# A state space stage on one core: where the scans' factors lie, who multiplies by C, and when TensorE makes the product with B

## The chip, the cores and the metric

The kernel runs on one core of a Trainium2 chip. The metric is the device time of one execution in microseconds (us), the median of several runs. A core has five engines that work side by side, each through its own queue in order: TensorE (PE, matrix products; its weight loads are listed as PEld), VectorE (DVE), ScalarE (ACT, functions such as exp), GpSimd (POOL) and SyncE (SP, which here issues the transfers). SBUF is the large on-chip memory, PSUM the small one that TensorE writes to. Semaphores order the engines among themselves.

## The reference

A two-layer model on an input of 16 sequences x 512 positions x 256 channels. The first layer is a feed-forward block with blockwise four-bit quantisation, a state space block and the same feed-forward block again; the second has two low-rank expert blocks around an attention block. The change lies in the state space block alone:

```python
xz = hidden_states @ W_in
x, z = jnp.split(xz, 2, axis=-1)            # 512 inner channels each
x = silu(conv(x) + conv_b)                  # 4 taps along the sequence
proj = x @ W_x
dt_low, Bm, Cm = ...                        # 16 columns each
dt = softplus(dt_low @ W_dt + b_dt)
A = -exp(A_log)                             # 512 x 16 states
def step(h, inputs):                        # along the 512 positions
    h = exp(dt_t[..., None] * A) * h + (dt_t * x_t)[..., None] * B_t[:, None, :]
    y = einsum('bds,bs->bd', h, C_t)
    return h, y
y = (ys + x * D) * silu(z)
return y @ W_out
```

## The kernel before

The stage goes through the 16 sequences (called batches here) one after the other. In each it walks over four groups c of 128 inner channels, called blocks c0 to c3, and in each block over eight steps k = 0 to 7; so a batch has 32 steps and the stage 512. A step holds 32 channels x 2 times 4 states on the 128 partitions, and 2 x 512 positions along the row: a tile of 128 x 1024. Steps go in pairs q = k // 2.

A step needs four things:

- **Factors** exp(dt A): two ACT instructions (`factors`, recorded by the helper at L480). They go to a tile that `factors_at` picks: one of two tiles in PSUM, `das` (da), or one of three in SBUF, `sides` (ds). Steps 2 to 5 take ds, the others da.
- **The product with B**, dt x B. For q = 0, 1 and 3 POOL makes it (`make_bx`, L483, tile bx in SBUF). For q = TQ = 2, steps 4 and 5, TensorE makes it in PSUM (`turn_bx`, 64 small products, rows da<-diag,dT), into the da tile that those steps do not need for factors.
- **The scan** h = factor x h + product, one VectorE instruction along the row (L979). After a scan of steps 4 and 5, VectorE sets the first column of the da tile back to zero (L985).
- **The product with C**: by POOL where `other` holds (steps 0, 1 and 3, and step 5 in c0 and c2; there h is the SBUF tile hs, and the result g is written at L483), else by VectorE (L486; there h is the one PSUM tile h).

TensorE adds the g of each pair over the states into the PSUM tile y (`accumulate`, rows y<-g,fold; the due step is written in `due`); for q = 0 the skip term D u comes first (y<-u,dskd). When the four pairs are in, VectorE multiplies y into zs (`finish_mult`) at step 0 of the next block.

Between all that, the preparation of the next batch is threaded in as a generator, `prepare`, which is advanced in each step up to the count in `PREPARED`: transposes of the input (xT), the products with W_in (p<-xT,w_in), the convolution as four products with diagonal matrices (p<-xp,cwd), silu of u, W_x, the transposes of the projection, W_dt, softplus of dt, POOL's dt u, the z half with its silu, transposes of dt u (dT), normalisation of the next input (xn), and the output product of the batch before (`out_half`, tile o). Each piece of TensorE's is copied from one PSUM buffer (tag mm) by ACT before the next piece may start. ACT changes its function tables for silu and softplus and back.

All engines take their instructions of this stage in the order in which the program records them (keep_in_program_order). The tables `FACTORS` (for which later step factors are made; the entries at the front of a step or at its end), `PRODUCTS` (for which later step bx is made), `PIECES` (how many of the eight copies of dt and dt u from DRAM, ds<-dd, are issued in a step) and `PREPARED` set that order by hand. SP issues the transfers: dd<-dt (to DRAM), ds<-dd (spread over states), bc<-bd (rows of B and C).

Of the kernel before, what the change touches and what calls it, by code (L numbers as in the profile page):

```python
# [9 lines left out]
F32 = mybir.dt.float32  # L10
# [6 lines left out]
P = 128  # L17
NB, SEQ, D = 16, 512, 256
# [19 lines left out]
def macaron_kernel(  # L38
# [430 lines left out]
    def mamba_phase(w, src, dst):  # L469
        with tc.tile_pool(name="m1", bufs=1) as m1, tc.tile_pool(  # L470
            name="m2", bufs=2
        ) as m2, tc.tile_pool(name="m_da", bufs=1, space=PSUM) as ps_da, tc.tile_pool(
            name="m_h", bufs=1, space=PSUM
        ) as ps_h, tc.tile_pool(name="m_y", bufs=1, space=PSUM) as ps_y, tc.tile_pool(
            name="m_ps", bufs=1, space=PSUM
# [12 lines left out]
            def pe(out, **kw):  # L488
                tc.keep_in_program_order(nc.tensor.matmul(out, **kw))  # L489
# [5 lines left out]
            a_neg, dskd, cwd, xps = w["a"], w["dskd"], w["cwd"], w["xp"]  # L495
            fold = w["fold"]
            NP = NS // 2
            NQ = NP // 2
            TQ = 2
# [4 lines left out]
            das = []  # L504
# [2 lines left out]
                nc.vector.memset(da[:, :, 0:1], 0.0)  # L507
                das.append(da)
            sides = []
            for i in range(3):  # L510
                da = m1.tile([P, 2, SEQ], F32, name=f"ds{i}")
                nc.gpsimd.memset(da[:, :, 0:1], 0.0)
                sides.append(da)
            diag = m1.tile([P, 4, NC4, P], F32, name="diag")

            state, xns, xos, zss, rows, norms, bds = {}, {}, {}, {}, {}, {}, {}
# [332 lines left out]
            def where(t):  # L849
                return t // STEPS, t // NP % NDC, t % NP  # L850

            PIECES = ((4, 4, 0, 0), (4, 2, 2, 0), (4, 2, 2, 0), (0, 0, 4, 4))
            PREPARED = (
                (2, 4, 4, 4, 4, 5, 7, 8), (9, 11, 11, 12, 12, 13, 14, 15),
                (16, 18, 18, 19, 21, 23, 25, 27), (30, 32, 33, 34, 35, 37, 39, 40),
            )
            FACTORS = ((1, 2), (2,), (2,), (2,), (), (1,), (1,), (1,))
            PRODUCTS = ((3,), (), (4,), (4,), (4,), (), (3,), (3,))
            bxs, ys, done = {}, [], []

            def run_later():
# [4 lines left out]
            def make_bx(t):  # L866
                b, c, k = where(t)
                if b < NB and k // 2 != TQ:
                    bx = m2.tile([P, 2, SEQ], F32, name="bx", tag="bx", bufs=3)
                    B = rows[b, k // 2][:, :1, :]  # L870
                    pool(
                        bx, spread[b, c, k % 2][:, :, 1, :],
                        B.to_broadcast([P, 2, SEQ]), ALU.mult,
                    )
                    bxs[t] = bx
# [13 lines left out]
            def turn_bx(t):  # L889
                b, c, k = where(t)  # L890
                if b < NB and k // 2 == TQ:
                    bx, dT = das[t % 2], state[b][1][c // 2]
                    for j in range(2):
                        at = c % 2 * P + 64 * (k % 2) + 32 * j
                        for n in range(NC4):
                            for i in range(4):
                                pe(
                                    bx[32 * i : 32 * i + 32, j, n * P : (n + 1) * P],
                                    lhsT=dT[:, n, at : at + 32], rhs=diag[:, i, n, :],
                                    start=True, stop=True,  # L900
                                )

            def accumulate(b, c, q, gs):
                if q == 0:
                    ys.append(ps_y.tile([P, SEQ], F32, name="y", tag="y"))
                    u = state[b][0][c // 2][:, c % 2, :]
                    for i in range(0, P, 32):
                        pe(
                            ys[0][i : i + 32, :], lhsT=dskd[i : i + 32, c, :],
                            rhs=u[i : i + 32, :], start=True, stop=False,  # L910
                        )
                for i in range(4):
                    pe(
                        ys[0][32 * i : 32 * i + 32, :], lhsT=fold,
                        rhs=gs[i // 2][:, i % 2, :], start=False, stop=(q == NQ - 1),
                    )
                if q == NQ - 1:
                    done.append((b, c, ys.pop()))
# [22 lines left out]
            for _ in range(4):  # L941
                next(rest)
            def factors_at(t):
                n, k = divmod(t, NP)
                return sides[(4 * n + k - 2) % 3] if 2 <= k <= 5 else das[k % 2]

            def factors(t):

                b, c, k = where(t)
                if b < NB:  # L950
                    q, p = k // 2, k % 2
                    da = factors_at(t)
                    for j in range(2):
                        g = 4 * c + 2 * p + j
                        act(
                            da[:, j, 1:], spread[b, c, p][:, j, 0, 1:],
                            AF.Exp, scale=a_neg[:, g, q : q + 1],
                        )

            factors(0)  # L960
            due, pair = {}, []
            for t in range(STEPS * NB):
                b, c, k = where(t)
                s = t % STEPS
                if s == 0:
                    prepared = 0
                    ahead = prepare(b + 1) if b + 1 < NB else close()
                    stat = stats(b + 2) if b + 2 <= NB else iter(())
                if k not in (1, 2, 3):
                    for n in FACTORS[k][:1]:  # L970
                        factors(t + n)

                other = k in (0, 1, 3) or k == 5 and c % 2 == 0
                if other:
                    h = m2.tile([P, 2, SEQ], F32, name="hs", tag="hs", bufs=2)
                else:
                    h = ps_h.tile([P, 2, SEQ], F32, name="h", tag="h")
                turned = k // 2 == TQ
                tc.keep_in_program_order(nc.vector.tensor_tensor_scan(  # L979
                    flat(h), flat(factors_at(t)), flat(das[k % 2] if turned else bxs.pop(t)),  # L980
                    0.0, op0=ALU.mult, op1=ALU.add,
                ))
                if turned:
                    tc.keep_in_program_order(
                        nc.vector.memset(das[k % 2][:, :, 0:1], 0.0)  # L985
                    )

                if t in due:
                    accumulate(*due.pop(t))
                if k == 2:  # L990
                    turn_bx(t + 2)
                if k == 4:
                    turn_bx(t + 1)
                if s == 2:
                    load_out(b - 1)
                if s == 17:
                    load(b + 2)
                if 20 <= s < 24:
                    next(stat, None)

                if k == (0, 0, 0, 2)[c]:
                    steps = fetch_steps(*divmod(b * NDC + c + 1, NDC))
                for _ in range(PIECES[c][k] if k < 4 else 0):
                    next(steps, None)
                run_later()
                if b and s == 0:
                    fetch(b, NQ - 1)
                if c == NDC - 1 and k in (2, 4, 6):
                    fetch(b + 1, k // 2 - 1)
                if t < 4:  # L1010
                    for _ in range(2):
                        next(rest, None)
                else:
                    for _ in range(min(3, PREPARED[c][k] - prepared)):
                        next(ahead, None)
                        prepared += 1
                for n in FACTORS[k][k in (0, 4, 5, 6, 7):]:
                    factors(t + n)
                g = m2.tile([P, 2, SEQ], F32, name="g", tag="g", bufs=4)
                C = rows[b, k // 2][:, 1:, :].to_broadcast([P, 2, SEQ])  # L1020
                if k == 0 and done:
                    finish_mult(*done.pop())
                if other:
                    pool(g, h, C, ALU.mult)
                else:
                    vec(g, h, C, ALU.mult)
                for n in PRODUCTS[k]:
                    make_bx(t + n)
                if s == STEPS - 3:
                    diags = diagonals(b + 1)  # L1030
                    next(diags, None)
                if s >= STEPS - 3:
                    next(diags, None)
                pair.append(g)
                if k % 2:
                    due[t + 1 + other] = (b, c, k // 2, pair)
                    pair = []
                if s == STEPS - 1:
                    for _ in ahead:
                        pass  # L1040
# [733 lines left out]
    with tc.tile_pool(name="mw", bufs=1) as mw:  # L1774
        with tc.tile_pool(name="x", bufs=1) as xp, tc.tile_pool(
            name="fw", bufs=1
# [23 lines left out]
    with tc.tile_pool(name="fw2", bufs=1) as fw, tc.tile_pool(  # L1800
        name="ln2", bufs=2
# [70 lines left out]
```

## Time and profile before

| what | value |
|---|---|
| median of 3 runs | 4398.21 us (4396.62 to 4403.94) |
| the profiled execution: its time, its span | 4394.14 us, 4392.4 us |
| state space stage, from the first scan to the last zs product | about 629.5 to 2573.5 us of the span |
| busy from 1500 to 1800 us (300 us) | PE 245.5, DVE 268.9, ACT 193.5, POOL 272.2 |
| granted clock of TensorE in that stretch | 0.94 |
| VectorE product g<-h,bc (x288) | 1.22 us |
| POOL bx<-ds,bc (x384), g<-hs,bc (x224), mean | 2.62 us, 2.77 us |
| ACT factor, one of two per step, da / ds | 0.69 / 0.71 us |
| ACT table load in the stage (x169) | 1.28 us |

The page lists the span in 40 slices with the busy tenths of each engine, the chain of waits, and groups of instructions by line with their mean time in ns and the idle time before them. In the stage no engine is at rest for long, so the average shares do not say which one sets the pace; the timeline of each engine, which lists instructions with start, duration and the idle time before them, does. The part after 2573 us (second feed-forward, experts, attention) is not touched.

### The profile page before, as it was taken

To read this page: it belongs to the slowest core of one execution; us is meant where nothing else is said; L and a number is where in the kernel's file an instruction comes from. 1 tells how busy PE (TensorE), PEld (TensorE's weight loads), DVE (VectorE), ACT (ScalarE), POOL (GpSimd) and SP (SyncE) were. 2 spreads that over 40 slices of the span, in tenths; PEclk is the share of its full clock that TensorE was granted. 3 is DMA by queue.
4 is the path that set the end of the run, shared out by engine and by line. 5 is a ranking of instruction groups with operands and counts; after the bars stand their busy time and mean duration, and the time that the engine had idled before them with its cause. 6 is when DMAs were issued, how large, how long until landed. Compare 5 with 4: busy or idle time off the path is not lost.

```text
span 4392.4 us, 68394 instructions
## 1 busy us (share of the span) xinstructions
PE 3838.7 (87%) x26498; PEld 2146.3 (49%) x26498; DVE 3791.1 (86%) x5002; ACT 2307.5 (53%) x3546; POOL 2067.6 (47%) x1688
## 2 busy tenths in 40 slices
PE   7999967878877877788788679999999999999989
PEld 4666633333333333333333346666664555555547
DVE  9999838999988888998999879999777888888776
ACT  4444336666666666666666534443434444444444
POOL 1000029999999999999999930000211111111122
PEclk9999979999999999999999889999999999999999
DMA  4000034544554454554445520000000000000002
GB/s 139 15 20 15 15 92 108 120 110 109 121 129 113 120 130 114 128 120 105 109 111 125 130 107 1 1 1 1 13 20 14 17 20 18 18 16 20 18 13 68
DMA packets 120472, 292.64 MB, mean 67 GB/s; under 512 B 30721, under 2 KB 50754, under 8 KB 120146
## 3 DMA queue, kind: packets, MB, share of 16 engines
q1 hardware_dynamic: 120146, 288.26, 26.0%
q8 instruction: 208, 3.41, 0.3%
q14 instruction: 118, 0.97, 0.1%
HBM read 209.26 MB, written 62.13 MB: 62 GB/s over the span
## 4 chain that ended last, share of the span: by engine, by line
PE 60%; ACT 13%; DVE 12%; DMA 6%; POOL 5%; issue 5%; SPq 1%; DVEq 0%; ACTq 0%; POOLq 0%
PE s L1201 10%; PE p L489 8%; PE g L289 7%; PE u L289 7%; PE o L325 7%; PE p L1201 4%; DVE h L979 4%; PE p L1204 3%; ACT da L480 3%; ACT L480 3%; PE o L1201 3%; DMA ds<-dd 3%; DMA bc<-bd 2%; PE y L489 2%; PE da L489 2%
## 5 line engine op out<-in xcount | busy, mean ns | idle before, releaser
L483 POOL TENSOR_TENSOR bx<-ds,bc 128x1024 f32<-128x1024 f32 x384 | 1002.1, 2617 | 61.0 <-DVE h L979 45.1
L483 POOL TENSOR_TENSOR g<-hs,bc 128x1024 f32<-128x1024 f32 x224 | 620.5, 2770 | 78.3 <-DVE hs L979 68.5
L1378 POOL TENSOR_SCALAR_AFFINE_SELECT eT<-eT 128x256 f32<-128x256 f32 (+1 forms) x384 | 189.0, 492 | 862.7 <-ACT eT L1372 862.7
L1372 ACT ACTIVATE eT<-s 128x768 f32<-128x768 f32 (+1 forms) x384 | 338.7, 882 | 417.1 <-PE s L1201 417.1
L480 ACT ACTIVATE da<-ds,a_neg 128x511 f32<-128x511 f32 x512 | 353.1, 690 | 273.3 <-DVE da L985 219.9
L1201 PE MATMUL s<-k,q 32*128 32x256 f32 (+3 forms) x2048 | 457.4, 469 | 7.8 <-DVE mx L1332 5.7
L489 PE MATMUL y<-g,fold 128*32 128x512 f32 x2048 | 354.6, 613 | 106.7 <-POOL g L483 64.5
L1332 DVE TENSOR_REDUCE mx<-s 128x2 f32<-128x1024 f32 (+3 forms) x512 | 410.2, 822 | 12.5
L1201 PE MATMUL s<-qm,k 32*128 32x512 f32 (+3 forms) x2048 | 383.8, 469 | 17.0 <-ACT eT L1372 11.9
L489 PE MATMUL p<-xT,w_in 128*128 128x512 f32 x500 | 314.5, 761 | 69.5 <-ACT dT L480 31.4
L979 DVE TENSOR_TENSOR_SCAN hs<-da,bx 128x1024 f32<-128x1024 f32 x128 | 292.3, 2284 | 85.4 <-ACT da L480 49.5
L486 DVE TENSOR_TENSOR g<-h,bc 128x1024 f32<-128x1024 f32 x288 | 351.0, 1219 | 16.5
L480 ACT ACTIVATE ds<-ds,a_neg 128x511 f32<-128x511 f32 x512 | 332.1, 710 | 19.6 <-DVE h L979 19.4
L1328 DVE TENSOR_TENSOR s<-s,mask 128x256 f32<-128x256 f32 (+1 forms) x384 | 199.0, 518 | 153.7 <-PE s L1201 143.7
L294 ACT ACTIVATE sl<-g 128x352 f32<-128x352 f32 x256 | 118.6, 465 | 384.6 <-PE g L289 373.4
L1529 POOL TENSOR_TENSOR g<-rs,v 128x4 f32<-128x4 f32 x64 | 13.1, 209 | 637.3 <-ACT rs L1526 551.7
L979 DVE TENSOR_TENSOR_SCAN h<-da,bx 128x1024 f32<-128x1024 f32 x128 | 293.9, 2296 | 15.6 <-ACT da L480 2.0
L489 PEld LDWEIGHTS da<-diag,dT 128*32 128x32 f32 x8192 | 236.8, 115 | 113.2 <-issue 60.4
L1201 PEld LDWEIGHTS s<-k,q 32*128 32x128 f32 x2048 | 205.8, 184 | 170.1 <-issue 92.6
L489 PE MATMUL p<-xp,cwd 128*128 128x512 f32 x480 | 231.0, 613 | 58.7 <-ACT xo L480 36.1
L979 DVE TENSOR_TENSOR_SCAN h<-ds,bx 128x1024 f32<-128x1024 f32 x64 | 229.7, 3589 | 58.2 <-ACT ds L480 58.2
L489 PE MATMUL da<-diag,dT 128*32 128x128 f32 x8192 | 272.0, 286 | 2.7 <-DVE hs L979 2.0
(289 smaller groups left out, 8156.8 us busy)
## 6 DMA issues: line engine op xcount, KB each, us to landing
ds<-dd SPq DMA_DIRECT2D x512, 256.0 KB, 5.8
bc<-bd SPq DMA_DIRECT2D x256, 128.0 KB, 6.5
dd<-dt SPq DMA_DIRECT2D x32, 1024.0 KB, 5.1
x<-_attn_hidden_states_dram SPq DMA_DIRECT2D x16, 512.0 KB, 6.2
xd<-x SPq DMA_DIRECT2D x16, 512.0 KB, 2.6
xo<-xd SPq DMA_DIRECT2D x16, 512.0 KB, 3.6
xe<-xo SPq DMA_DIRECT2D x16, 512.0 KB, 2.9
x<-xe SPq DMA_DIRECT2D x16, 512.0 KB, 10.2
```

The source lines that it names most:

```text
L289: nc.tensor.matmul(dst, lhsT=xT[:, k, c * P : (c + 1) * P], rhs=w[:, k, f0 : f0 + HF], start=(k == 0), stop=(k == KD - 1),)
L325: last = nc.tensor.matmul(o, lhsT=hT[:, f, :], rhs=wdT[:, f, :], start=(f == 0), stop=False)
L480: return tc.keep_in_program_order(nc.scalar.activation(out, in_, func, **kw))
L483: tc.keep_in_program_order(nc.gpsimd.tensor_tensor(out, in0, in1, op=op))
L486: tc.keep_in_program_order(nc.vector.tensor_tensor(out, in0, in1, op=op))
L489: tc.keep_in_program_order(nc.tensor.matmul(out, **kw))
L979: tc.keep_in_program_order(nc.vector.tensor_tensor_scan(flat(h), flat(factors_at(t)), flat(das[k % 2] if turned else bxs.pop(t)), 0.0, op0 ...
L1201: tc.keep_in_program_order(nc.tensor.matmul(out, **kw))
L1328: nc.vector.tensor_tensor(own, own, const["mask"][:, :w].unsqueeze(1).to_broadcast([P, 2, w]), op=ALU.add)
L1332: nc.vector.tensor_reduce(mx[:, t, 2 * pair : 2 * pair + 2, RM], s[:, :, off : off + (t + 1) * P], axis=AX.X, op=ALU.max,)
L1372: const["exp"] = nc.scalar.activation(eT[:, 2 * pair : 2 * pair + 2, e0 : e0 + w], s[:, :, :w], AF.Exp)
L1378: nc.gpsimd.affine_select(out=own, in_=own, compare_op=ALU.is_ge, fill=0.0, base=0, pattern=[[0, 2], [0, n], [1, P]] if n > 1 else [[0, 2] ...
```

## The change

- `sides` has two tiles instead of three, and only steps 4 and 5 use them. Steps 2 and 3 now have their factors in the PSUM tiles da, like steps 0, 1, 6 and 7; so each scan has one operand in PSUM (da as factor, or as product with B in steps 4 and 5).
- Factors are made one step ahead (`FACTORS`), the ones for steps 4 and 5 at the ends of steps 2 and 3.
- The product with C of step 3 goes to VectorE and that of step 6 to POOL: `other` is steps 0, 1, 6 and 5 in c0 and c2.
- bx has four buffers instead of three, and `PRODUCTS` makes those of steps 6 and 7 together in step 2, and those of steps 0 and 1 of the next block together in step 4.
- `turn_bx` for steps 4 and 5 is recorded in steps 3 and 4, right behind the scan and ahead of `accumulate`. The products for D u leave `accumulate` and stand in step 1 (`add_du`); the sum for q = 0 comes in step 3.
- `PREPARED` advances the preparation by other counts; in c3 the copies ds<-dd of the next block are issued in steps 1 and 2 instead of 2 and 3.

```diff
             sides = []
-            for i in range(3):
+            for i in range(2):
                 da = m1.tile([P, 2, SEQ], F32, name=f"ds{i}")
...
-            PIECES = ((4, 4, 0, 0), (4, 2, 2, 0), (4, 2, 2, 0), (0, 0, 4, 4))
+            PIECES = ((4, 4, 0, 0), (4, 2, 2, 0), (4, 2, 2, 0), (0, 4, 4, 0))
             PREPARED = (
-                (2, 4, 4, 4, 4, 5, 7, 8), (9, 11, 11, 12, 12, 13, 14, 15),
-                (16, 18, 18, 19, 21, 23, 25, 27), (30, 32, 33, 34, 35, 37, 39, 40),
+                (2, 3, 4, 4, 4, 5, 6, 8), (9, 10, 11, 11, 11, 13, 14, 15),
+                (16, 17, 18, 18, 18, 21, 24, 27), (29, 30, 32, 32, 32, 35, 37, 40),
             )
-            FACTORS = ((1, 2), (2,), (2,), (2,), (), (1,), (1,), (1,))
-            PRODUCTS = ((3,), (), (4,), (4,), (4,), (), (3,), (3,))
+            FACTORS = ((1,), (1,), (1, 2), (), (), (1,), (1,), (1,))
+            PRODUCTS = ((3,), (), (4, 5), (), (4, 5), (), (), (3,))
...
-                    bx = m2.tile([P, 2, SEQ], F32, name="bx", tag="bx", bufs=3)
+                    bx = m2.tile([P, 2, SEQ], F32, name="bx", tag="bx", bufs=4)
...
+            def add_du(b, c):
+                ys.append(ps_y.tile([P, SEQ], F32, name="y", tag="y"))
+                u = state[b][0][c // 2][:, c % 2, :]
+                for i in range(0, P, 32):
+                    pe(
+                        ys[0][i : i + 32, :], lhsT=dskd[i : i + 32, c, :],
+                        rhs=u[i : i + 32, :], start=True, stop=False,
+                    )
+
             def accumulate(b, c, q, gs):
-                if q == 0:
-                    ys.append(ps_y.tile([P, SEQ], F32, name="y", tag="y"))
...
             def factors_at(t):
-                n, k = divmod(t, NP)
-                return sides[(4 * n + k - 2) % 3] if 2 <= k <= 5 else das[k % 2]
+                return (sides if t % NP // 2 == TQ else das)[t % 2]
...
-                if k not in (1, 2, 3):
-                    for n in FACTORS[k][:1]:
-                        factors(t + n)
-
-                other = k in (0, 1, 3) or k == 5 and c % 2 == 0
+                for n in FACTORS[k][:1]:
+                    factors(t + n)
+
+                other = k in (0, 1, 6) or k == 5 and c % 2 == 0
...
+                if k in (3, 4):
+                    turn_bx(t + 1)
+                if k == 1:
+                    add_du(b, c)
                 if t in due:
                     accumulate(*due.pop(t))
-                if k == 2:
-                    turn_bx(t + 2)
-                if k == 4:
-                    turn_bx(t + 1)
...
-                if k == (0, 0, 0, 2)[c]:
+                if k == (0, 0, 0, 1)[c]:
...
-                for n in FACTORS[k][k in (0, 4, 5, 6, 7):]:
+                for n in FACTORS[k][1:] if k != 3 else (2,):
                     factors(t + n)
...
-                    due[t + 1 + other] = (b, c, k // 2, pair)
+                    due[t + 1 + (k == 1 or other)] = (b, c, k // 2, pair)
```

More of the change, by code (lines that the diff above doesn't have):

```diff
@@ L901, in turn_bx @@
                                 )
-            def accumulate(b, c, q, gs):
-                if q == 0:
-                    ys.append(ps_y.tile([P, SEQ], F32, name="y", tag="y"))
[L906 to L911, printed above, removed]
+            def add_du(b, c):
[6 more added lines that the diff above has]
+                    )
+            def accumulate(b, c, q, gs):
                 for i in range(4):
```

## The prediction

> **Terms.** A batch is 32 steps, four blocks c0 to c3 of steps 0 to 7. F(k) is the pair of exponentials of step k on ScalarE (ACT). I time a block from the start of its step-2 scan to that of the next block. All times in us.
>
> **What bounds the kernel now.** First the page by slices: in the state space stage (about 628 to 2570 of 4392.4) VectorE (DVE) and GpSimd (POOL) are both near nine tenths, so a gain there need not be lost to a third engine on average. Then the groups by line, for what one scan costs:
>
> ```profile
> L979 DVE TENSOR_TENSOR_SCAN hs<-da,bx 128x1024 f32<-128x1024 f32 x128 | 292.3, 2284 | 85.4 <-ACT da L480 49.5
> ...
> L979 DVE TENSOR_TENSOR_SCAN h<-da,bx 128x1024 f32<-128x1024 f32 x128 | 293.9, 2296 | 15.6 <-ACT da L480 2.0
> L979 DVE TENSOR_TENSOR_SCAN h<-ds,bx 128x1024 f32<-128x1024 f32 x64 | 229.7, 3589 | 58.2 <-ACT ds L480 58.2
> ```
>
> The same scan takes 2.29 when its factors lie in PSUM (da) and 3.59 when both operands lie in SBUF (ds, bx). The timeline shows why: beside such a scan a POOL product takes 4.3 instead of 2.36. hs<-ds,bx has a mean of 3.50 in the groups by shape. So steps 2 and 3 lose 1.30 + 1.21 = 2.5 per block, 160 over 64 blocks. That is the prize.
>
> Then the timeline, for where VectorE stands still. Both cuts are of one batch, ACT's before VectorE's:
>
> ```profile
> 1443.72 1.28 ACT L480 ACT_TABLE_LOAD   x1 [2.96 <-DVE da L985]
> 1445.02 1.42 ACT L480 ACTIVATE da<-ds,a_neg 128x511 f32<-128x511 f32 x2
> 1446.37 0.58 ACT L480 ACTIVATE proj<-p 128x512 f32<-128x512 f32 x1
> 1447.69 0.22 ACT L480 ACTIVATE bT<-p 128x64 f32<-128x64 f32 x1 [0.74 <-PE p L737]
> ...
> 1460.62 1.06 ACT L480 ACTIVATE dt<-dt 128x1024 f32<-128x1024 f32 x1
> 1461.70 1.28 ACT L598 ACT_TABLE_LOAD   x1
> 1462.99 0.30 ACT L480 ACTIVATE r<-mv,eps 128x4 f32<-128x4 f32 x1
> 1463.32 0.20 ACT L480 ACTIVATE r<-r 128x4 f32<-128x4 f32 x1
> 1463.43 1.32 ACT L480 ACTIVATE ds<-ds,a_neg 128x511 f32<-128x511 f32 x2
> ```
>
> ```profile
> 1441.24 2.27 DVE L979 TENSOR_TENSOR_SCAN h<-ds,da 128x1024 f32<-128x1024 f32 x1
> ...
> 1464.84 3.45 DVE L979 TENSOR_TENSOR_SCAN h<-ds,bx 128x1024 f32<-128x1024 f32 x1 [3.73 <-ACT ds L480]
> ...
> 1489.51 2.29 DVE L979 TENSOR_TENSOR_SCAN hs<-da,bx 128x1024 f32<-128x1024 f32 x1 [0.43 <-POOL bx L483]
> ...
> 1495.62 2.29 DVE L979 TENSOR_TENSOR_SCAN hs<-da,bx 128x1024 f32<-128x1024 f32 x1 [3.25 <-ACT da L480]
> ```
>
> ACT runs without a pause worth naming from the end of scan 4 of c2 (1443.5) to F(2) of c3 (1464.75), and VectorE waits 3.73 for it; the same at the batch's end (3.25). The step-2 scans start at 1404.80, 1432.74, 1464.84, 1497.83: c1 lasts 27.9, c2 32.1, c3 33.0. Over the full batches the means are c0 28.6, c1 27.9, c2 32.1, c3 32.5, together 121.1. So c0 and c1 are set by VectorE, c2 and c3 by the chain through ACT.
>
> **The change, part by part.** *Scans.* Steps 2 and 3 fall from 3.59 and 3.50 to the 2.29 of the da rows: -2.5 a block where VectorE sets the pace. Product counts stay: step 3's moves from POOL to VectorE (1.22) and step 6's the other way (2.36 uncontended). VectorE alone then needs per block five scan-and-product pairs of about 3.7 (1542.82 to 1546.58 is 3.76, 3.6 when another buffer follows), and scans without product 2.2, 2.85 with the zs product: 24.3 in c0 and c2, 25.5 in c1 and c3. POOL needs 38 products of 2.33 and about 10 of small work, 99 a batch: not the bound.
>
> *Lookahead.* F(2) and F(3) now go to da, so each F(k) waits for scan k-2; before, the three ds buffers let them run earlier. Only F(4) and F(5) run early now, and behind them ACT waits idle for scan 4. Since ACT is in order, what follows F(6) in its queue starts late. I count this from the order in which the changed program holds ACT's instructions, with the pitches of the rows above.
>
> c2, zero at its scan 2: two pairs of 3.75 and scan 4 of 2.3 end at 9.8; F(6) starts 0.2 later (before: 1443.51 to 1443.72). Now u (0.69), load (1.30) and the silu of u (1.07) stand *behind* F(6); before they ran ahead of it, in ACT's 2.96 pause. The chain: F(6) 1.35, u, load, silu, load, F(7) = 7.06; proj with TensorE's transposes 1.32 (1446.37 to 1447.69), bT, TensorE's dt product and dt 1.44 + 0.60, F(0) 1.35: 11.8; dt 0.69, load 1.30, softplus 0.96, dt 0.69, load 1.29, F(1) 1.35: 18.05; dt 0.69, load, softplus, load 3.66, r 0.44, F(2) 1.41: 24.25. Scan 2 of c3 starts at 10.0 + 24.25 = 34.3, against 32.1: **+2.2**. Scan 1 now waits too (about 3.4), and queued behind it is step 2.
>
> c3: F(3) now comes before zs, so the transposes, the second w_in product (3.71 at half clock, 1466.69 on) and the product with B (3.1) end 1.3 later: scan 4 at 10.2 instead of 8.88. F(6) from 12.6, then zs, dT 1.9, load, silu, load 3.67, F(7) to 21.0, zs and dT 1.8, F(0) to 24.1. Then zs waits for TensorE (2.0 after dT), 24.9, dT 26.2, four normalisations 26.7 to 28.8, load, silu, load 3.67, F(1) 1.4: scan 1 at 34.0, scan 2 at 36.2, against 33.0 in that batch, 32.5 in the mean: **+3.7**. Before, two of the normalisations and the last zs stood ahead of F(0).
>
> c0: TensorE begins after the same long idle. The two w_in products took 3.78 each at a clock of 0.50, then the B product 2.34: scan 4 came at 10.71. The D products (1.06) now stand ahead of them: 11.1. The rest is 16.95. The convolution's four taps (3.70) now stand in one piece before the last y sum, so the zs product waits about 1.05: 29.1, against 28.6: **+0.5** (28.1 without that wait, 30 if the D products run at half clock).
>
> c1: VectorE alone 25.5; the silu of u ahead of F(0) may cost 0.5 and a late y sum 1.2, so 25.5 to 27.5. I take the middle, 26.5: **-1.4**.
>
> Sum +5.0 a batch, with both ends +3 to +7. Fifteen batches: +75. The last batch has no preparation of another on ACT; there its blocks fall from 26.3 to 26.6 to the 24.3 and 25.5: -6. Stage +69.
>
> *Costed at nothing.* The earlier copies of steps to ds (c3's eight transfers move from steps 2 and 3 to 1 and 2 on SP's queue, the last four past a bc copy and the second dd copy): their first use, bx of the next block, is needed some 24 later; without that cover each late transfer would cost its 5.8. The fourth bx buffer only relaxes POOL. POOL's dt products wait about 6 for the later softplus, and the bx behind them is still 4 early; once that is gone scan 2 waits.
>
> **A rule weighed.** The clock in the trace is 0.50 from 1496 to 1504 and 0.64 to 1508, though TensorE worked most of it from 1496.09. The Trainium skill, "TensorE: Matmul & The Clock Gate", section "What's actually happening", puts the full clock after about 3.4 us of sustained work. By the rule the second w_in product would run at full clock and c0 be 1.8 shorter, 27 over fifteen batches, 42 in place of 69; the rows have it at half clock, and they decide.
>
> **The rivals.** *A, faster: ACT catches up and VectorE keeps its gain.* ACT's busy share of the stage is two thirds, which speaks for it; its unbroken chain between 1443.7 and 1464.8 speaks against. It decides where F(1) and F(2) of c3 and c0 are no later after scan 4 than now (21.3 in c2): c0 28.1, c1 25.5, c2 31, c3 31 give 115.6, -5.5 x 15 - 6 = -89, 4305 in the profile; at most the whole 160, 4234. Chance 0.17. *B, TensorE becomes the bound.* It is busy 245 of 300 already, in order, with one buffer for the projections; if its clock falls in more places, c0 30.5, c1 28.5, c2 35.5, c3 38 make 132.5: +11.4 x 15 - 6 = +165, 4559. For it: the longer idle stretch in c3 and before c0. Against: full clock in c1 and c2 now. Chance 0.10. *C, the two effects cancel* within 0.2%, or a da scan contends with POOL after all (128 and 128 rows at 2.29 say no): 4398, 0.03.
>
> **How the numbers follow.** My forecast has 0.70: 4394.1 (the profiled execution; its span 4392.4 and 1.7 around it) + 69 = 4463. The median of the runs is 4.1 above that execution: 4467. Its own ends, +3 and +7 a batch, give 4394 + 4 + 39 = 4437 and 4497. For 8 in 10 I go from 4405, leaving out A, to 4530, leaving out most of B. A measurement here tells about 0.2% (9 us) from nothing. Faster takes A less a little, 0.16; same 0.04; slower 0.80.
>
> **What would show it.** Right: every scan near 2.29, no POOL product near 4.3, DVE idle before hs<-da in step 1 of c3 and c0 of 3.4 and 6.5 for ACT, step 2 of c3 with its wait kept, blocks of 29, 26.5, 34, 36. Wrong: those waits for ACT at step 1 missing or no longer than now (A), a clock share below 0.9 through c1 (B), or the scan rows above 2.5.

## The result: 1.5% slower, with other blocks than forecast

The changed kernel takes 4465.65 us (median of 4 runs, 4464.81 to 4467.38) against 4398.91 (4396.62 to 4403.94) before: ratio 1.0151, 95% interval 1.0133 to 1.0168. The forecast was 4467, so the size is nearly exact, but part of that is luck: of the four blocks of a batch, c0 came out 2.5 shorter than forecast and c3 and c1 1.9 and 0.9 longer, and these errors cancel in the sum.

The page of the changed kernel, its head and the groups that answer to the scan rows of before (busy time and mean of one in ns, then the idle time ahead of them and what ended it; the scan, L979 before, stands in line 978 here, the setting to zero, L985 before, in 984):

```profile
span 4464.0 us, 68345 instructions
...
PE 3800.6 (85%) x26498; PEld 2151.8 (48%) x26498; DVE 3642.5 (82%) x5002; ACT 2309.5 (52%) x3543; POOL 1843.8 (41%) x1687
...
L483 POOL TENSOR_TENSOR bx<-ds,bc 128x1024 f32<-128x1024 f32 x384 | 900.1, 2364 | 61.7 <-DMA ds<-dd 58.4
...
L978 DVE TENSOR_TENSOR_SCAN hs<-da,bx 128x1024 f32<-128x1024 f32 x192 | 438.5, 2284 | 138.2 <-ACT da L480 105.6
```

The change does what it says: every group of scans has a mean of 2.28 to 2.30, the POOL product 2.36 instead of a mean of 2.62, and busy time falls by 149 on VectorE (3791.1 before) and by 224 on POOL (2067.6). The span grew all the same. What grew is VectorE's waiting. The view of waits for VectorE in the stage (640 to 2560; total us, how often, longest), first before, then after:

```profile
DVE h L979 <- ACT ds L480: 63.3, 17, 5.1
DVE hs L979 <- ACT da L480: 49.5, 17, 3.2
DVE hs L979 <- ACT ds L480: 28.7, 15, 2.3
DVE h L979 <- PE da L489: 16.3, 14, 1.9
```

```profile
DVE zs L486 <- PE y L489: 137.5, 58, 3.9
DVE hs L978 <- ACT da L480: 105.6, 46, 6.0
DVE h L978 <- POOL bx L483: 60.6, 16, 3.8
DVE h L978 <- PE da L489: 52.1, 29, 2.9
```

The first line of the second cut is new: the zs product, almost never kept waiting before (2.1 in all), now waits 137.5 for TensorE's y sum. By blocks (scan 2 to the next block's scan 2, means over the full batches):

| block | before | forecast | after |
|---|---|---|---|
| c0 | 28.5 | 29.1 | 26.6 |
| c1 | 28.0 | 26.5 | 27.4 |
| c2 | 32.1 | 34.3 | 34.2 |
| c3 | 32.5 | 36.2 | 38.1 |
| sum | 121.1 | 126.1 | 126.35 |

Both long blocks show how. ACT's timeline of the changed kernel from the end of c2 (start, duration, instruction, in brackets the idle time before it):

```profile
1597.76 1.41 ACT L480 ACTIVATE da<-ds,a_neg 128x511 f32<-128x511 f32 x2 [5.87 <-DVE da L984]
1599.11 0.67 ACT L480 ACTIVATE u<-p,cb 128x512 f32<-128x512 f32 x1
1599.80 1.28 ACT L480 ACT_TABLE_LOAD   x1
1601.09 1.06 ACT L480 ACTIVATE u<-u 128x1024 f32<-128x1024 f32 x1
1602.17 1.28 ACT L480 ACT_TABLE_LOAD   x1
1603.46 1.41 ACT L480 ACTIVATE da<-ds,a_neg 128x511 f32<-128x511 f32 x2
1604.81 0.58 ACT L480 ACTIVATE proj<-p 128x512 f32<-128x512 f32 x1
...
1614.43 1.42 ACT L480 ACTIVATE da<-ds,a_neg 128x511 f32<-128x511 f32 x2
...
1618.83 1.28 ACT L598 ACT_TABLE_LOAD   x1
...
1620.57 2.73 ACT L480 ACTIVATE da<-ds,a_neg 128x511 f32<-128x511 f32 x4
```

F(6), the first line, waits 5.87 for scan 4's tile; then the silu of u and its two loads run behind it, and from there ACT has hardly a gap until F(2) at 1620.57, the start of the last line. VectorE at the ends of the two long blocks (c3 into c0 of the next batch, then c2 into c3):

```profile
1525.78 0.69 DVE L486 TENSOR_TENSOR zs<-zs,y 128x512 f32<-128x512 f32 x1 [3.94 <-PE y L489]
1531.63 2.29 DVE L978 TENSOR_TENSOR_SCAN hs<-da,bx 128x1024 f32<-128x1024 f32 x1 [5.17 <-ACT da L480]
...
1615.36 0.69 DVE L486 TENSOR_TENSOR zs<-zs,y 128x512 f32<-128x512 f32 x1 [3.40 <-PE y L489]
...
1622.05 2.30 DVE L978 TENSOR_TENSOR_SCAN h<-da,bx 128x1024 f32<-128x1024 f32 x1 [3.81 <-POOL bx L483]
```

TensorE ahead of the first of these zs products, at the end of c3:

```profile
1518.19 3.78 PE L489 MATMUL p<-xT,w_in 128*128 128x512 f32 x4 [0.69 <-ACT dT L480]
1522.75 1.09 PE L760 MATMUL p<-ident,dt 128*128 128x128 f32 x4 [0.78 <-ACT zs L480]
1523.77 1.94 PE L489 MATMUL y<-g,fold 128*32 128x512 f32 x8
```

Two of the named releasers mislead. The y sum before 1615.36 was held up on TensorE by a dt product that itself waited 1.68 for ACT's copy of dt, so that wait is ACT's too; F(1) itself (the line at 1614.43) ended at 1615.85, just ahead of scan 1 at 1615.96. And POOL's bx for the scan at 1622.05 was finished at 1617.4; what ended last is the first half of ACT's last line above, F(2) (two of its four instructions, about 1.4 from 1620.57).

### The profile page after: what moved, and what is told of

It is laid out like the page before. It is cut to its first block, busy times and chain, and to the rows that moved or that the text cites. A ratio compares the mean times of both kernels' runs of the same rounds, so it can differ in the third digit from the quotient of the medians.

```text
span 4464.0 us, 68345 instructions
## 1 busy us (share of the span) xinstructions
PE 3800.6 (85%) x26498; PEld 2151.8 (48%) x26498; DVE 3642.5 (82%) x5002; ACT 2309.5 (52%) x3543; POOL 1843.8 (41%) x1687
## 4 chain that ended last, share of the span: by engine, by line
PE 38%; DVE 12%; ACT 7%; DMA 3%; issue 2%; POOL 2%; SPq 0%; DVEq 0%; ACTq 0%; POOLq 0%
PE s L1200 10%; PE p L1200 4%; PE g L289 3%; PE u L289 3%; PE o L325 3%; PE p L1203 3%; DVE h L978 3%; PE o L1200 3%; DVE hs L978 2%; ACT da L480 2%; PE p L489 2%; PE r L1200 2%; ACT L480 2%; DVE mx L1331 2%; DMA ds<-dd 1%
## 5 line engine op out<-in xcount | busy, mean ns | idle before, releaser
L483 POOL TENSOR_TENSOR bx<-ds,bc 128x1024 f32<-128x1024 f32 x384 | 900.1, 2364 | 61.7 <-DMA ds<-dd 58.4
L480 ACT ACTIVATE da<-ds,a_neg 128x511 f32<-128x511 f32 x768 | 528.1, 689 | 456.4 <-DVE da L984 238.9
L483 POOL TENSOR_TENSOR g<-hs,bc 128x1024 f32<-128x1024 f32 x224 | 528.0, 2357 | 299.1 <-DVE hs L978 221.0
L978 DVE TENSOR_TENSOR_SCAN hs<-da,bx 128x1024 f32<-128x1024 f32 x192 | 438.5, 2284 | 138.2 <-ACT da L480 105.6
L978 DVE TENSOR_TENSOR_SCAN h<-da,bx 128x1024 f32<-128x1024 f32 x192 | 439.2, 2288 | 99.5 <-POOL bx L483 60.6
L489 PE MATMUL y<-g,fold 128*32 128x512 f32 x2048 | 298.1, 632 | 28.7 <-POOL g L483 15.4
L978 DVE TENSOR_TENSOR_SCAN h<-ds,da 128x1024 f32<-128x1024 f32 x96 | 220.4, 2296 | 62.7 <-PE da L489 52.1
L489 PE MATMUL da<-diag,dT 128*32 128x128 f32 x8192 | 256.8, 278 | 17.0 <-DVE h L978 17.0
L489 PEld LDWEIGHTS p<-xT,w_in 128*128 128x128 f32 x500 | 106.8, 237 | 275.9 <-issue 86.7
```

Source lines behind the costliest of these rows:

```text
L480: return tc.keep_in_program_order(nc.scalar.activation(out, in_, func, **kw))
L483: tc.keep_in_program_order(nc.gpsimd.tensor_tensor(out, in0, in1, op=op))
L978: tc.keep_in_program_order(nc.vector.tensor_tensor_scan(flat(h), flat(factors_at(t)), flat(das[k % 2] if turned else bxs.pop(t)), 0.0, op0 ...
```

## The experiments

All edits are against the changed kernel unless said. The kernel before, measured beside them, had medians of 4396.6 to 4399.4. Where no interval is given, the kernel has one time.

### The counts and the scans, taken apart

The change has two large parts: where factors lie (with all that follows), and the new counts of `PREPARED`. The first run keeps the change but takes back the counts:

```diff
-                (2, 3, 4, 4, 4, 5, 6, 8), (9, 10, 11, 11, 11, 13, 14, 15),
-                (16, 17, 18, 18, 18, 21, 24, 27), (29, 30, 32, 32, 32, 35, 37, 40),
+                (2, 4, 4, 4, 4, 5, 7, 8), (9, 11, 11, 12, 12, 13, 14, 15),
+                (16, 18, 18, 19, 21, 23, 25, 27), (30, 32, 33, 34, 35, 37, 39, 40),
```

> The changed kernel with the counts (PREPARED) of the kernel before: the silu of u and its table loads stand again in front of F(6) of c2, and two normalisations and the last zs in front of F(0) at the batch's end; factors stay in da, one step ahead. Theory (the loss is where ACT's other work stands, not the factors in da): c2 falls from 34.2 to about 31.2 us, c3 from 38.1 to about 34.5, c0 and c1 stay within 1 of 26.6 and 27.4; about 119.5 to 120.5 a batch instead of 126.3, so 4360 to 4390 us. Rival 1 (the loss is the shorter lookahead, factors of steps 2 and 3 waiting for scans 0 and 1): no change, 4455 to 4475. Rival 2 (TensorE's order is what was gained by the new counts): c1, c2 and c3 grow by a product of 2 us each where pieces come between the two products with B, 4500 or more.

Measured: 4337.87, ratio to before 0.9861 (0.9844 to 0.9877). The direction of the theory held and the gain was larger than expected: c2 31.6 and c3 31.75. c0 grew by 1.7, to 28.3, more than the 1 allowed for; c1 is 26.8. Its ACT timeline at the same place in the batch:

```profile
1535.17 1.28 ACT L480 ACT_TABLE_LOAD   x1
1536.47 1.06 ACT L480 ACTIVATE u<-u 128x1024 f32<-128x1024 f32 x1
1539.41 1.28 ACT L480 ACT_TABLE_LOAD   x1 [1.88 <-DVE da L984]
1540.70 1.42 ACT L480 ACTIVATE da<-ds,a_neg 128x511 f32<-128x511 f32 x2
1542.56 0.60 ACT L480 ACTIVATE proj<-p 128x512 f32<-128x512 f32 x1 [0.45 <-PE p L489]
```

The silu of u now fills the pause ahead of F(6), and proj follows F(6) after 1.86 instead of 7.05. The second run is the other half: the kernel before, with only its `PREPARED` replaced by the new counts.

> The kernel before with the counts (PREPARED) of the changed one and nothing else. Theory: ACT's chain from the end of scan 4 of c2 to F(2) of c3 grows by u, a load and silu, 3.1 us, and the batch's end by about 3: 121.1 goes to about 127, the time to 4470 to 4510 us. Rival (with three ds tiles of lookahead the counts do not matter): 4385 to 4410.

Measured: 4528.99, more than expected: c3 grew by 5.6, c2 by 1.8, and c1, which the theory had left out, by 2.8. The four corners:

| | old counts | new counts | counts cost |
|---|---|---|---|
| before (factors of steps 2, 3 in ds) | 4399 | 4529 | +130 |
| after (factors in da) | 4338 | 4466 | +128 |
| the change's other parts give | -61 | -63 | |

So in these four the two parts add up (4529 is a single time). The slowdown is the counts, whichever scans they go with; it is not the shorter lookahead of the factors, which is in both corners of the lower row.

The third run asks which of the other parts gives the 63. It puts the factors of steps 2 and 3 back into ds, and leaves order, lookahead and counts as changed:

```diff
-                return (sides if t % NP // 2 == TQ else das)[t % 2]
+                return (sides if 2 <= t % NP <= 5 else das)[t % 2]
```

> The changed kernel with the factors of steps 2 and 3 in the two SBUF tiles that steps 4 and 5 use, so scans 2 and 3 have both operands in SBUF again; order and counts of the changed kernel. It measures the price of the contention alone. Theory: scans 2 and 3 go from 2.29 to 3.2 to 4.3 us and POOL's products beside them to 4.3; c0 and c1 are then some 2.5 longer each, c2 and c3 0 to 2.5 each as their waits for ACT take some of it: 5 to 9 a batch, 4540 to 4600 us. Rival (what the scans gained had been hidden behind waits in all blocks): 4455 to 4480.

Measured: 4534.76, 69 more than the changed kernel and just under the expected window. Its scan group by shape:

```profile
L978 DVE TENSOR_TENSOR_SCAN h<-ds,bx 128x1024 f32<-128x1024 f32 x128 | 392.4, 3066 | 70.0 <-ACT ds L480 55.0 <-POOL bx L483 4.5 <-issue 2.4
```

The scan with two operands in SBUF is back at 3.07, and POOL's products at 2.69 and 2.77. That alone accounts for all that the change gains at fixed counts; order, moved products and shorter lookahead together come to about nothing (4528.99 with the kernel before at these counts, 4534.76 here), which does not show that each of them is nothing.

How the two engines get in each other's way can be read from the kernel before. VectorE's scans of steps 2 and 3 in one block:

```profile
1527.07 4.17 DVE L979 TENSOR_TENSOR_SCAN h<-ds,bx 128x1024 f32<-128x1024 f32 x1
...
1532.42 3.13 DVE L979 TENSOR_TENSOR_SCAN hs<-ds,bx 128x1024 f32<-128x1024 f32 x1
```

and POOL beside them:

```profile
1526.72 2.36 POOL L483 TENSOR_TENSOR bx<-ds,bc 128x1024 f32<-128x1024 f32 x1
1529.03 4.37 POOL L483 TENSOR_TENSOR g<-hs,bc 128x1024 f32<-128x1024 f32 x1
1533.36 4.34 POOL L483 TENSOR_TENSOR bx<-ds,bc 128x1024 f32<-128x1024 f32 x1
```

The first product began before the scan and took its usual 2.36, to 1529.08. The scan ended 2.16 after that, the next product 2.16 after the scan, and so on in turn with 2.15 each. So by these rows neither side runs at a lower speed: whoever comes second makes no headway until the instruction of the other is over, and then needs little less than its usual time. The whole trace before agrees: 119 of the 128 scans with both operands in SBUF are long, and each ends 2.14 or more (median 2.15) after the product of POOL beside which it began; each of the 97 long products of POOL ends 2.13 to 2.18 after such a scan. The Trainium skill, "SBUF — State Buffer", section "Who interferes with whom", says that a VectorE instruction with two SBUF inputs contends with a GpSimd instruction that reads SBUF, and calls the contention on the ports that the two share an exclusive lock. These rows agree with both: the mean scan grows from 2.29 to 3.59 and POOL's product from 2.36 to 4.3 because each waits for the other in turn.

### Small parts, alone

D u back into `accumulate`, out of step 1:

```diff
+                if q == 0:
+                    add_du(b, c)
...
-                if k == 1:
-                    add_du(b, c)
```

> The changed kernel with the four D products back in the sum of q = 0 (step 3, behind the first product with B) instead of step 1. Theory: at the batch's start, where TensorE runs at half clock, they stand no longer ahead of the two w_in products (1.93 us): c0 1 to 2 shorter, c1 to c3 within 0.5: 4435 to 4455 us. Rival (the sum of q = 0 and the second product with B then come a step's part too late): scan 5 waits about 1 in each block, 4490 to 4530.

Measured: 4467.62, a miss: nothing was gained, and c0 stayed at 26.5. TensorE's timeline at the start of a batch, first as changed, then with D u moved back:

```profile
1532.10 1.12 PE L635 MATMUL p<-ident,xn 128*128 128x128 f32 x4 [5.25 <-ACT xT L480]
1533.15 1.93 PE L489 MATMUL y<-u,dskd 32*32 32x512 f32 x8
1535.01 2.87 PE L489 MATMUL p<-xT,w_in 128*128 128x512 f32 x4
```

```profile
1530.44 1.12 PE L635 MATMUL p<-ident,xn 128*128 128x128 f32 x4 [5.20 <-ACT xT L480]
...
1532.26 3.47 PE L489 MATMUL p<-xT,w_in 128*128 128x512 f32 x4 [0.70 <-ACT xT L480]
```

After 5.2 of idle time somebody has to run at half clock. As changed, the D products do (1.93 instead of 1.06) and w_in takes 2.87; without them w_in takes it (3.47). So here the moved products fill time that the slow clock costs anyway.

The old order of bx, each made by itself again:

```diff
-            PRODUCTS = ((3,), (), (4, 5), (), (4, 5), (), (), (3,))
+            PRODUCTS = ((3,), (), (4,), (4,), (4,), (), (3,), (3,))
```

> The changed kernel with the old order of POOL's products with B (PRODUCTS), four buffers kept. Theory: POOL has slack in each block, so nothing: 4455 to 4475 us. Rival (scan 2 of c3, whose last releaser in the profile is POOL's bx, is set by POOL's order): c2 and c3 move by 1 or more, 4440 or less, or 4485 or more.

Measured: 4465.49, no effect, as expected. The old choice of who multiplies by C in steps 3 and 6:

```diff
-                other = k in (0, 1, 6) or k == 5 and c % 2 == 0
+                other = k in (0, 1, 3) or k == 5 and c % 2 == 0
```

> The changed kernel with the products with C as before: step 3 on POOL, step 6 on VectorE. Theory: in c0 and c3 scan 4 waits for TensorE, which hides VectorE's product of step 3; in step 6 it is not hidden in c0: c0 1 to 1.5 longer, the other blocks within 0.5: 4475 to 4500 us. Rival (POOL's product of step 3 holds the sum of pair 1 and so TensorE back): c1 and c2 longer as well, 4510 or more.

Measured: 4473.2, 7.5 more, a little less than expected, and not by the blocks that were expected: c0 and c1 are 0.8 and 1.3 longer, c2 is 1.75 shorter and c3 0.4 shorter. In the sum it matters little here who multiplies by C.

### The counts, place by place

If u's silu behind F(6) is what makes c2 long, moving it alone should mend c2:

```diff
-                (16, 17, 18, 18, 18, 21, 24, 27),
+                (16, 17, 18, 18, 20, 21, 24, 27),
```

> The changed kernel with one move: u and the silu of u of c2 (with its two table loads) are recorded in step 4 instead of 5, so in front of F(6) in ACT's queue; all other counts as changed. Theory (in-order ACT, work behind F(6) that could stand ahead of it): ACT's chain from the end of scan 4 to F(2) loses u, one load and silu, 3.06 us: c2 34.2 goes to 31.2, other blocks within 0.5; 4466 - 16 x 3 = 4418 us (4410 to 4430). Rival (ACT is not the bound there, TensorE's products for the projection and dt are): c2 34 to 34.5 and 4455 to 4470.

Measured: 4463.94, a miss; c2 is 34.4. The silu did move, but the counts then leave TensorE's next piece, the transposes of proj, to step 6. TensorE's timeline there:

```profile
1602.01 0.66 PE L737 MATMUL p<-ident,proj 128*128 128x128 f32 x4 [3.20 <-ACT proj L480]
1602.97 1.78 PE L489 MATMUL p<-proj,w_dt 128*128 128x512 f32 x2 [0.31 <-ACT bT L480]
1605.53 2.08 PE L489 MATMUL p<-proj,w_dt 128*128 128x512 f32 x2 [0.78 <-ACT dt L480]
1607.54 1.94 PE L489 MATMUL y<-g,fold 128*32 128x512 f32 x8
```

TensorE idles 3.20, the granted clock falls (0.91 from 1600, 0.50 from 1604 to 1608), and the pieces of the chain take 1.78, 2.08 and 1.94, where at full clock they take 1.12, 1.12 and 1.06: 2.5 more in all. ACT for its part gained 1.7 and not the 3.06 expected. Counted from scan 2, proj's copy stands at 15.2 instead of 16.9, because the second table load still starts only when scan 4 lets F(6) go, and F(7) then waits 1.29 for scan 5. What ACT gained, TensorE lost. So the next run moves silu and proj together:

```diff
-                (16, 17, 18, 18, 18, 21, 24, 27),
+                (16, 17, 18, 18, 21, 23, 24, 27),
```

> The changed kernel with u and its silu of c2 ahead of F(6), as in the run before that failed, and with the projection's copy and bT moved up by a step too (step 5), so that TensorE is not left idle ahead of proj. In that run TensorE stood idle 3.2 us there, its clock fell to 0.50 from 1604 to 1608, and the dt products took 1.78 and 2.08 us instead of 1.12. Theory (ACT's chain, joined to a cold TensorE in that run): clock 1.00 in steps 5 to 7 of c2, c2 31.0 to 31.8 instead of 34.2, other blocks within 0.5: 4410 to 4430 us. Rival (it was not the clock; ACT's chain is as long wherever u stands): c2 33.5 or more, 4450 or more.

Measured: 4415.83, c2 30.45. The same stretch of TensorE:

```profile
1578.68 0.66 PE L737 MATMUL p<-ident,proj 128*128 128x128 f32 x4 [0.69 <-ACT proj L480]
1579.64 1.13 PE L489 MATMUL p<-proj,w_dt 128*128 128x512 f32 x2 [0.31 <-ACT bT L480]
1581.56 1.12 PE L489 MATMUL p<-proj,w_dt 128*128 128x512 f32 x2 [0.79 <-ACT dt L480]
```

0.69 of idle time in place of 3.20, and full clock. But not all of the gain is the clock: proj's copy no longer stands behind F(7) and comes 12.7 after scan 2, 2.5 earlier than in the run before. No run separates the two parts of the 3.95 between these runs. One row of counts is worth 50 of the 128. Next, the row of c3 alone, old against new:

```diff
-                (29, 30, 32, 32, 32, 35, 37, 40),
+                (30, 32, 33, 34, 35, 37, 39, 40),
```

> The changed kernel with the old counts in block c3 alone (two normalisations, the last zs and dT ahead of F(0), the silu of the first zs half in step 4 ahead of F(6)). Theory: c3 falls from 38.1 by 3.5 to 6.5, c0 grows by 0 to 1.5 since TensorE is longer idle before it, c1 and c2 as they are: 4370 to 4420 us; with the move of c2 it makes up most of the 128 us between the changed kernel and its version with all old counts (4338). Rival (c3's length is set by the y sum on TensorE, for which the zs product waited 3.9 us): c3 stays above 37, 4450 or more.

Measured: 4436.8, less than expected. c3 fell to 33.6 as it should, but c1 rose to 30.0: of the 14 full batches it is 27.4 in three, where the granted clock in that block is 1.00, 29.9 in four (0.89) and 31.1 in seven (0.84). TensorE's same product in c1 of two batches:

```profile
1434.11 1.98 PE L489 MATMUL p<-xT,w_in 128*128 128x512 f32 x4 [2.94 <-ACT u L480]
```

```profile
935.55 3.78 PE L489 MATMUL p<-xT,w_in 128*128 128x512 f32 x4 [2.94 <-ACT u L480]
```

The idle time ahead of it is 2.94 in all 14; the product behind it takes 1.98 in the short blocks, 2.6 to 2.8 in the middle ones and 3.78 in the long ones. So the length of the pause alone does not decide whether the clock falls; what does was not found.

### Counts made for the changed kernel

With u's silu ahead of F(6), proj in step 5 and the copies of c3 and c0 spread out, in all four rows:

```diff
+                (2, 3, 4, 4, 5, 6, 7, 8), (9, 11, 11, 12, 14, 15, 16, 17),
+                (18, 18, 18, 19, 21, 23, 25, 27), (30, 32, 33, 35, 36, 38, 40, 40),
```

> The changed kernel with counts set by the theory: everything heavy on ACT (silu of u twice, silu of the first zs half, the second xp copy in c0) in steps 3 and 4, where ACT otherwise idles some 4 to 6 us behind F(5); all four normalisations ahead of F(0) and only the last silu between F(0) and F(1). Theory: c0 27, c1 26 to 26.5, c2 31.3, c3 30.5 to 31.5, 115 to 116 a batch: 4290 to 4310 us. Rival (TensorE, busy in order, sets c0 and c1 already, so pieces that come earlier only queue): 4325 to 4350, with the DVE idle before zs<-zs,y for PE longer than in the version with old counts (86.6 us).

Measured: 4303.66, ratio to before 0.9785 (0.9769 to 0.9801). This is inside the expected window and beats both kernels: blocks 25.4, 27.8, 32.0, 30.9, so c0 came out shorter than expected and c1 and c2 longer. Do these counts need the change? The kernel before with them:

> The kernel before with the counts of the retimed version (4304 us) and nothing else: scans 2 and 3 in SBUF, contended. Theory (gain by the scans and gain by the counts add): c2 and c3 shorter by 1 to 2 together, c0 and c1 stay 28 with VectorE: 118 to 120 a batch, 4355 to 4385 us. Rival (the counts pay only with the scans in PSUM, because the contention fills the same gaps): 4390 or more.

Measured: 4394.76. The theory fell: the counts alone give the old kernel nothing that can be told (its scans with ds stay at 3.40 and 3.68), the change alone at old counts gives 61, and both together 95. Here the parts do not add. The rival's number held; its reason, that the contention fills the same gaps, was not tested. Last, the row of c2 that did best joined to the retimed rows of c0 and c3:

```diff
+                (2, 3, 4, 4, 5, 6, 7, 8), (9, 10, 11, 11, 11, 13, 14, 15),
+                (16, 17, 18, 18, 21, 23, 24, 27), (30, 32, 33, 35, 36, 38, 40, 40),
```

> The changed kernel with the best row found for each block: c0 and c3 of the retimed version, c1 as changed, c2 of the run with u, its silu and the projection moved up. Theory (blocks add, since each one's length is set by its own queue of ACT and TensorE): 25.4 + 27.4 + 30.5 + 30.9 = 114.2 a batch against 116.05 retimed, so 4304 - 15 x 1.9 = 4275 us (4265 to 4290). Rival (TensorE carries the lag of one block into the next, as between c0 and c1 where the y sum is late): 4300 to 4320, the gain of c2 given back in c3 or c1.

Measured: 4303.43, ratio 0.9786 (0.9770 to 0.9803), the same as the retimed one; the rival held. In the traced execution (4309.95, the longest of the four) c2 keeps its 30.5, but c3 is 32.4 instead of 30.9 and c1 28.2 instead of 27.8. Its waits of VectorE in the stage:

```profile
DVE h L978 <- PE da L489: 74.8, 43, 4.2
DVE h L978 <- POOL bx L483: 59.0, 16, 3.8
DVE hs L978 <- ACT da L480: 52.6, 45, 2.6
```

The first wait, for TensorE's product with B, was 56.9 in the retimed kernel: VectorE waits about as often as there (43 times, 44 there) but longer. The difference lies in c3, where scan 4 starts 10.6 after scan 2 and not 9.1, as much as c3 has grown. The product with B ahead of that scan, first in a c3 of 33.0 in the joined kernel, then in one of 30.6 in the retimed kernel:

```profile
1085.02 3.19 PE L489 MATMUL da<-diag,dT 128*32 128x128 f32 x64
```

```profile
1200.78 1.95 PE L489 MATMUL da<-diag,dT 128*32 128x128 f32 x64
```

In the joined kernel TensorE had stood idle 3.15 at the start of this block, in the retimed one 2.83, and the granted clock came back later (0.50 still from 1085.1 to 1087.1, 1.00 already from 1200.0). And c1, whose row is that of the changed kernel, is 27.4 in eight full batches and 28.8 or more in six, again behind the same pause of 2.94. So part of what the row of c2 gained was lost to TensorE's clock. Whether another place for the pieces of the preparation on TensorE would keep both gains, or one for the last softplus behind F(2), was not tried.

## Why the prediction was right, step by step

- **Scans.** As costed: 2.28 to 2.30 for the scans, and the longest of POOL's products bx and g takes 2.43, none near 4.3. The prize was put at 160; at the new counts the factors alone are worth 69 in the time (the run with factors in ds), all parts but the counts 61 at the old counts, 63 at the new and 91 at the retimed ones (4394.76 to 4303.66). The rest does not show in the time, since VectorE then waits for ACT and TensorE instead.
- **Lookahead.** The counting of ACT's queue was right, its heading was not. The text put the late chain to F(k) waiting for scan k-2. The four corners show that the counts alone cost 128 to 130, also with the long lookahead of before. What the text itself described, the silu of u standing behind F(6), is an edit of `PREPARED`.
- **c2, +2.2.** Forecast 34.3, measured 34.2. Scan 1's wait of 3.4 came as 3.40 ahead of the zs product, by TensorE's name but through ACT's copy; step 2 kept its wait, 3.81. The run with silu and proj moved took c2 to 30.45, so the chain named sets this block; the silu alone, moved without proj, did not shorten it (34.4).
- **c3, +3.7.** Mechanism right, term too small: 38.1 instead of 36.2. Scan 4 came earlier than forecast (9.35 after scan 2, not 10.2), and in the batch shown F(0) ended 24.0 after scan 2, as forecast (24.1). From there on the sum is too short: scan 1 started 36.2 after scan 2, not 34.0, and the wait at step 1 is 9.1 (3.94 and 5.17), not 6.5. The missing part is a fall of the clock that the sum did not have, to 0.54 from 1516 and 0.50 from 1520: the third w_in product took 3.78 instead of 1.98 and the transposes behind it 1.09 instead of 0.66. That is 2.2 in ACT's chain to F(1), the whole of the difference. The y sum took 1.94 instead of 1.06, which moves time from the second of the two waits to the first but does not hold F(1).
- **c0, +0.5.** Forecast 29.1, measured 26.6. The tail was right (16.95 and 1.05 make 18.0; measured 17.95). Wrong was the start: scan 4 at 8.7, not 11.1, since the two w_in products took 2.87 and 1.99, not 3.78 each, and the product with B 1.95, not 2.34, while the D products ahead of them took 1.93, not 1.06. The granted clock was 0.50 from 1532 to 1536, 0.59 to 1537 and 1.00 from there, after work had begun at 1532.10: full clock came back after about 4.7, an estimate from these windows. Here the Trainium skill ("TensorE: Matmul & The Clock Gate", section "What's actually happening", full clock after about 3.4 us of sustained work) comes closer than the rows of before that I preferred, though the measured 4.7 is longer. In the rows of before the pieces were separated by short waits (0.69); whether that is the difference was not tested.
- **c1, -1.4.** Forecast 26.5, measured 27.4, close to the upper end that I gave: the late y sum (zs waits 1.22) and the silu ahead of F(0) (scan 0 waits 0.75 for ACT) both cost.
- **Costed at nothing.** The bx order shows no effect when undone. The earlier copies were not undone alone. POOL does wait for them in the changed kernel (58.4 of the 61.7 in its bx line above), but in the batch shown the products that waited were done by 1512.56, 7 before scan 0 at 1519.55, the first that needs one, so no scan waited for them there; with the old counts and the same copies POOL waits 3.6 for them in the whole stage.
- **Rivals.** A, that ACT catches up, is false for these counts; with the old ones the time falls to 4338, so a table of 32 numbers decided between A and the forecast. B needed the clock below 0.9 through c1; it is 1.00 there. C fell with the time.

## What to carry to other kernels

On an engine that works in order, put work that waits for nothing ahead of an instruction that waits for a gate: here a silu with the load before it, taken ahead of the gated F(6), and the copy of the next product, taken ahead of the gated F(7), made a block of 34.2 us 3.8 shorter; the silu alone did not. Retime the hand-made order together with the change that frees an engine, and measure both corners: the change without its counts gave 61, the retimed counts alone nothing, both 95. And in a chain that crosses TensorE, an idle stretch of some 3 us can cost twice, since the next pieces may run at half clock: they did after 3.20 in the run with the silu alone, and after 2.94 in some batches of the run with the old row of c3 and not in others.

## What the runs showed that I had not expected

- A table load ahead of a gated exponential did not use the pause: in the cut with the old counts the load at 1539.41 starts only after 1.88 idle, when the gate opens, and the exponential comes 1.29 later.
- Products placed where the clock is at half speed anyway can be free: D u cost 0.87 more at its new place and the block did not get longer.
- A block cannot be judged alone: the c3 row taken back made c3 4.5 shorter and c1 2.6 longer, and with the best c2 row c2 became 1.5 shorter and c3 1.4 longer than in the retimed kernel.
